# The recurrence of a four-layer kernel: conv by projection and diagonal taps, step sizes a group ahead with an operand in PSUM, keys in even slots

## The chip, the cores and the metric

The kernel runs on one core of one Trainium2 chip. Its time is the time of one execution in device microseconds (us). Five engines work side by side, each in the order of its own queue: PE multiplies matrices, DVE, ACT and POOL work element by element, SP issues DMAs. Data lies in SBUF (128 partitions) and in PSUM, which PE writes.

## What is computed

Four layers with residuals follow one another on x (4 sequences of 512 tokens, width 512, float32): a selective state-space layer driven by a context of width 256, a mixture of experts (64 experts, 8 per token), cross attention with 16 heads, and a feed-forward layer with quantized operands. The change concerns the first:

```
xc = causal_conv(in_proj_w @ ctx, conv_w)      # 4 taps per channel, 512 channels
u  = silu(xc + conv_b)
dt_lo, Bm, Cm = split(x_proj_w @ u)
delta = softplus(dt_proj_w @ dt_lo + dt_proj_b)
for each position:                             # 16 states per channel
    state = state * exp(delta * A) + (delta * u) * Bm
    y = sum over the states of state * Cm
out = (y + D * u) * silu(z)
```

The result is added to x; z comes from the normalized x. The keys and values of the attention layer depend on the context alone, so their projections are computed in part beside the first layer.

## The kernel before

The first layer is `ssm_phase`. Its instructions are written in the order in which each engine takes them; no scheduler changes it. The loop over `q` has 128 passes: sequence b (4, called batches), group of 128 channels c (4), pair of states i (8). One pass is called a slot here, and s is the slot within a batch (0 to 31). What a slot issues, in order:

- POOL multiplies du by the row of B for slot q + 2 (`inputs`, L518, into one of three buffers dBu).
- ACT makes exp(delta A) for slot q + 1 (`decays`, L529), into one of two PSUM buffers dA. Twice in a batch (`early`) it goes into an SBUF buffer ahead of its turn.
- DVE runs the scan along the positions (`scan`, L543); the product with the row of C is done by POOL for i = 0, 2, 4 and by DVE otherwise (L544, into one of three buffers hc).
- PE transposes the product of the slot before onto the PSUM tile yT, which adds up over the states (`sums`, L549). At i = 2 of the next group DVE multiplies yT by the gate (`result`, L583) and adds it to x (L586: on POOL, in the last batch on DVE). There is one yT.

Beside this each slot holds a piece of other work. `values` (PE L500, ACT L506, a store from SP) projects the values of attention in every second slot. The keys go through class `Keys`: `task` (PE L1227), `evict` (ACT L1236, L1237, a store), `squares` (PE L1247), `take` (ACT L1259, a store); 3, 6, 6 and 16 of them lie in the four batches, and nine more are computed later, in the expert layer (`key_tasks`).

`ahead` and `ahead_ends` prepare the next batch. For slots 0 to 15 PE computes the conv, two matmul calls a slot, from weights in which projection and taps are folded together (L320; a matmul call on float32 is two instructions in the profile). Then come the statistics of x (DVE), the norm (POOL L405 to L410), silu of u with two loads of ACT's tables (slot 17), the projection to B, C and dt (`project` L424, `take_project` L429), its store to DRAM by L430 and, from slot 26, the loads that spread its rows over the partitions (`rows`, L436, eight of 1024 KB a batch). In slots 19 to 28 the step sizes of all four groups of the next batch are made: `dt` (PE L443), `steps_a` (three on ACT), `steps_ln` (ACT L459, L462), `steps_b` (DVE L468, L469, L471) and `step_du` (POOL L479, L482). delta and du therefore have five buffers each, and u has six.

For batch 0 there is no time ahead: it projects by `conv_0`, applies the taps on DVE (`taps_0`, L351), and before and between makes the folded weights: `fold` scales the weights (DVE L371, ACT L369), `turn_fold` transposes them on PE (L378), `take_fold` copies them (L385, L387), `store_fold` writes them to DRAM, 512 KB for each group of channels; `load_wcv` (L310) reads them again for each batch. Its steps after the first group are in slots 1 to 12.

Of the kernel before, what the change touches and what calls it, by code (L numbers as in the profile page):

```python
# [24 lines left out]
ALU = mybir.AluOpType  # L25
# [215 lines left out]
def ssm_phase(ctx, cm, x_all, w, kv, router_stats):  # L241

    tc, nc = cm.tc, cm.nc
    pool = {n: ctx.enter_context(tc.tile_pool(name=f"a_p{n}", bufs=n)) for n in (1, 2, 3, 4, 5, 6)}
# [17 lines left out]
    def load_ctx(b, again=False):  # L264

        t = pool[2].tile([P, KC, S + DC - 1], F32, name="ctxb")
        nc.vector.memset(t[:, :, 0:DC - 1], 0.0)
        nc.sync.dma_start(t[:, :, DC - 1:],
                          w["ctxT"][:, b * S:(b + 1) * S].rearrange("(k p) s -> p k s", p=P))
        if again:  # L270
            st[b]["ctx"] = t
            return
        st[b] = dict(ctx=t, w=[], u=[], gz=[], delta=[], du=[], bb=[], cb=[],
                     mv=small.tile([P, NC, 2], F32, name="mv"))

    winT = pool[4].tile([P, KC, DM], F32, name="winT", tag="bb")
    nc.sync.dma_start(winT, w["in_proj_wT"].rearrange("(k p) e -> p k e", p=P))
    load_ctx(0)
    winE = pool[4].tile([P, NC, CTX], F32, name="winE", tag="cb")
    nc.sync.dma_start(winE, w["in_proj_w"].rearrange("(c p) k -> p c k", p=P))  # L280
# [24 lines left out]
    wcv_dram = dp.tile([NC, P, KC, DC, P], F32, name="wcv_dram")  # L305


    def load_wcv(b, c):
        t = pool[2].tile([P, KC, DC, P], F32, name="wcvc")
        nc.sync.dma_start(t, wcv_dram[c])  # L310
        st[b]["w"].append(t)

    def conv(b, c, parts):
        s = st[b]
        if 0 in parts:
            s["pin"] = ps.tile([P, S], F32, name="pin")
        for i in parts:
            k, j = divmod(i, DC)

            nc.tensor.matmul(s["pin"], s["w"][c][:, k, j, :], s["ctx"][:, k, j:j + S], start=i == 0,  # L320
                             stop=i == KC * DC - 1)

    def take_conv(b, c):
        u = pool[6].tile([P, S], F32, name="u")
        nc.scalar.activation(u, st[b]["pin"], AF.Identity, bias=vecs["conv_b"][:, c:c + 1])
        st[b]["u"].append(u)


    def conv_0(c):
# [3 lines left out]
        for k in range(KC):  # L333
            nc.tensor.matmul(pin, winT[:, k, c * P:(c + 1) * P], s["ctx"][:, k, DC - 1:],
                             start=k == 0, stop=k == KC - 1)

    def take_conv_0(c):
        s = st[0]
        xin = s["xin", c] = pool[2].tile([P, S + DC - 1], F32, name="xin", tag="wcvc")
        nc.gpsimd.memset(xin[:, 0:DC - 1], 0.0)  # L340
        pin = s.pop(("pin", c))
        nc.scalar.copy(xin[:, DC - 1:], pin)
        u = pool[6].tile([P, S], F32, name="u")
# [4 lines left out]
    def taps_0(c):  # L348
        xin, u = st[0].pop(("xin", c)), st[0]["u"][c]
        for j in range(DC - 1):  # L350
            nc.vector.scalar_tensor_tensor(u, xin[:, j:j + S], vecs["conv_w"][:, c, j:j + 1], u,  # L351
                                           ALU.mult, ALU.add)
# [5 lines left out]

    wsc = {}

    def fold(c):
        t = wsc[c] = pool[3].tile([P, DC, CTX], F32, name="wsc", tag="dBu" if c < 3 else "hc")
        for j in range(DC):
            scale = vecs["conv_w"][:, c, j:j + 1]
            if c == 3:
                nc.scalar.activation(t[:, j, :], winE[:, c, :], AF.Copy, scale=scale)  # L369
            else:  # L370
                nc.vector.tensor_scalar(t[:, j, :], winE[:, c, :], scale, None, ALU.mult)  # L371

    def turn_fold(c):
        t = wsc.pop(c)
        pt = wsc[c] = pda.tile([P, KC, DC, P], F32, name="pwcv", tag="dA")
        for k in range(KC):
            for j in range(DC):
                nc.tensor.transpose(pt[:, k, j, :], t[:, j, k * P:(k + 1) * P], cm.ident)  # L378

    def take_fold(c):  # L380
        pt = wsc.pop(c)
        t = wsc[c] = pool[4].tile([P, KC, DC, P], F32, name="wcv", tag="bb" if c % 2 else "cb")
        for k in range(KC):
            if c < 2:
                nc.scalar.copy(t[:, k], pt[:, k])  # L385
            else:
                nc.vector.tensor_copy(t[:, k], pt[:, k])  # L387

    def store_fold(c):
        nc.sync.dma_start(wcv_dram[c], wsc.pop(c))  # L390
# [21 lines left out]
    def silu_gz(b):  # L412
        s = st[b]
        for c in range(NC):
            gz = pool[5].tile([P, S], F32, name="gz")
# [30 lines left out]
    def steps_a(b):  # L446

        s = st[b]
        pdt = s.pop("pdt")
        s["e"], s["wt"] = (pool[1].tile([P, S], F32, name=n) for n in ("e", "wt"))  # L450
        s["relu"] = pool[5].tile([P, S], F32, name="delta")
# [4 lines left out]
    def steps_ln(b):  # L456

        s = st[b]
        nc.scalar.activation(s["wt"], s["e"], AF.Identity, bias=cm.ones[:, 0:1])  # L459
        s["ln"] = (pool[5].tile([P, S], F32, name="ln", tag="gz") if b == 0 else  # L460
                   ps.tile([P, S], F32, name="ln", tag="pin"))
        nc.scalar.activation(s["ln"], s["wt"], AF.Ln)  # L462

    def steps_b(b):

        s = st[b]
        e, wt, ln = s["e"], s["wt"], s["ln"]
        nc.vector.scalar_tensor_tensor(e, wt, 1.0, e, ALU.subtract, ALU.subtract)  # L468
        nc.vector.tensor_tensor(e, ln, e, ALU.subtract)  # L469
        delta = s.pop("relu")  # L470
        nc.vector.tensor_tensor(delta, delta, e, ALU.add)  # L471
        s["delta"].append(delta)

    def step_du(b):
# [3 lines left out]
        du = pool[5].tile([P, S], F32, name="du")  # L478
# [16 lines left out]
    def values(b, n, Wv):  # L495
        g, kc = divmod(n, S // P)
        pv = pvs[b, n] = ps.tile([P, HG * HD], F32, name="pv")
        at = slice(DC - 1 + kc * P, DC - 1 + (kc + 1) * P)
# [22 lines left out]
    def decays(q, early=False):  # L521

        if q < len(seq) and q not in dAs:
            b, c, i = seq[q]
            dAs[q] = (pool[2].tile([P, 2, S], F32, name="dA", tag="wcvc") if early else
# [55 lines left out]
    def result(b, c):  # L581
# [3 lines left out]

        (nc.vector if b == B - 1 else nc.gpsimd).tensor_tensor(xv, xv, t, ALU.add)  # L586

    def ahead(b, s):

        if s % 4 == 0 and 4 <= s <= 16:  # L590
            take_conv(b, s // 4 - 1)
        if s < 16:
            conv(b, s // 4, (s % 4 * 2, s % 4 * 2 + 1))
        if s in (4, 8):
            load_wcv(b, s // 4 + 1)
        if 12 <= s < 16:
            stats(b, s - 12)
        if s == 16:
            norm(b)
        if s == 17:  # L600
            silu_u(b)
        if s == 18:
            project(b)
        if s == 19:
            take_project(b)
        if s in (20, 22, 24, 26):
            steps_a(b)
        if s in (21, 23, 25):
            dt(b, (s - 19) // 2)
        if s in (22, 24, 26, 28):  # L610
            step_du(b)
        if s in (21, 23, 25, 27):
            steps_ln(b)
        if s == 29:
            silu_gz(b)
        if s == 20 and b + 1 < B:
            load_ctx(b + 1)
        if s == 20 and b + 1 == B:
            load_ctx(0, again=True)
        if s in (26, 28, 30, 31):  # L620
            rows(b, (26, 28, 30, 31).index(s))

    def ahead_ends(b, s):

        if s in (16, 28):
            decays((b - 1) * SL + s + 2, early=True)
        if s in (29, 31) and b + 1 < B:
            load_wcv(b + 1, (s - 29) // 2)
        if s == 19:
            dt(b, 0)  # L630
        if s in (21, 23, 25, 27):
            steps_b(b)
# [3 lines left out]
    def key_bank(shape, name):  # L636
# [1782 lines left out]
```

## Time and profile before

| | us |
|---|---|
| median of 3 runs | 2706.72 |
| lowest and highest | 2701.98 to 2717.91 |
| profiled execution | 2719.86 |
| its span in the profile | 2718.1 |
| end of the last product of the recurrence (L544) in the span | 577.1 |
| busy time of PE, DVE, POOL, ACT up to 577 | 492, 493, 476, 366 |
| mean granted clock of PE up to 577, and after | 0.90, 0.97 |

The profile is one execution. Busy time of an engine is the time in which it had an instruction in work; it says nothing on whether others waited for it. A window line gives, for a stretch of the span, the busy time and the number of instructions of each engine, then the granted clock of PE (1.00 is full), the share of time in which the DMA engines were busy, and what they moved. A line of an operation gives the least, the median and the greatest duration in ns. In a timeline line an idle time and what ended it stand in brackets.

### The profile page before, as it was taken

To read this page: it belongs to the slowest core of one execution; us is meant where nothing else is said; L and a number is where in the kernel's file an instruction comes from. 1 tells how busy PE (TensorE), PEld (TensorE's weight loads), DVE (VectorE), ACT (ScalarE), POOL (GpSimd) and SP (SyncE) were. 2 spreads that over 40 slices of the span, in tenths; PEclk is the share of its full clock that TensorE was granted. 3 is DMA by queue.
4 is the path that set the end of the run, shared out by engine and by line. 5 is a ranking of instruction groups with operands and counts; after the bars stand their busy time and mean duration, and the time that the engine had idled before them with its cause. 6 is when DMAs were issued, how large, how long until landed. Compare 5 with 4: busy or idle time off the path is not lost. (4 is left out here: it accounts for less than half of the span.)

```text
span 2718.1 us, 29941 instructions
## 1 busy us (share of the span) xinstructions
PE 2526.6 (93%) x10151; PEld 1432.6 (53%) x10151; DVE 1524.8 (56%) x2575; ACT 1237.6 (46%) x2355; POOL 1174.4 (43%) x1085
## 2 busy tenths in 40 slices
PE   5989797987799999999998799999999999999987
PEld 2545454654455666666674354445555555555543
DVE  5897989976322244344324555556665666544446
ACT  5666666655322222232322344444555455545543
POOL 4888888960333344443435423223332333211112
PEclk8979798988899999999998999999999999999999
DMA  6253535432656567879876444233332343222100
GB/s 247 90 196 104 199 105 183 125 124 98 196 189 210 185 221 219 288 264 321 283 222 215 130 134 128 90 100 110 125 101 86 109 128 113 75 76 66 51 31 20
DMA packets 199358, 404.67 MB, mean 149 GB/s; under 512 B 30611, under 2 KB 72147, under 8 KB 195104
## 3 DMA queue, kind: packets, MB, share of 16 engines
q1 hardware_dynamic: 156574, 249.33, 27.6%
q0 software_dynamic: 40576, 153.19, 17.7%
q8 instruction: 83, 1.36, 0.2%
q10 hardware_dynamic: 2050, 0.18, 0.1%
q14 instruction: 75, 0.61, 0.1%
HBM read 320.70 MB, written 81.92 MB: 148 GB/s over the span
## 5 line engine op out<-in xcount | busy, mean ns | idle before, releaser
L1981 DVE TENSOR_REDUCE mx<-psc 128x1 f32<-128x512 f32 x256 | 176.8, 691 | 459.6 <-PE psc L1978 459.6
L1327 PE MATMUL pg<-xT,wg 128*128 128x284 f32 (+12 forms) x1536 | 404.7, 408 | 1.4 <-ACT xT L1314 1.1
L1327 PEld LDWEIGHTS pg<-xT,wg 128*128 128x128 f32 x1536 | 285.4, 196 | 86.7 <-issue 36.9
L518 POOL TENSOR_TENSOR dBu<-bb,du 128x1024 f32<-128x1024 f32 x128 | 318.5, 2512 | 21.3 <-DVE dA L543 13.6
L1984 ACT ACTIVATE e<-psc,mx 128x512 f32<-128x512 f32 x256 | 176.1, 688 | 310.7 <-DVE mx L1981 310.4
L1268 POOL DMA_INDIRECT xg<-xn_dram,tok x168 | 172.8, 1028 | 219.5 <-PE pt L1311 177.4
L1978 PE MATMUL psc<-kT,qT 128*128 128x512 f32 x512 | 266.2, 602 | 1.0 <-ACT qT L1972 1.0
L2005 PE MATMUL po<-eT,v 128*128 128x512 f32 x512 | 233.2, 598 | 10.4 <-ACT eT L1999 10.3
L1944 PE MATMUL pq<-Wq,xnT 128*128 128x512 f32 x512 | 235.9, 604 | 0.7 <-DMA k_dram<-k_kT 0.7
L2014 PE MATMUL px<-Wo,oT 128*128 128x512 f32 x512 | 230.2, 592 | 0.0
L529 ACT ACTIVATE dA<-delta,negA 128x512 f32<-128x512 f32 x256 | 176.8, 694 | 79.1 <-DVE hc L544 62.2
L1998 PEld LDWEIGHTS pet<-ident,e 128*128 128x128 f32 x1024 | 127.0, 141 | 146.4 <-issue 119.6
L1955 POOL TENSOR_SCALAR qms<-qms 128x4 f32<-128x4 f32 x64 | 24.8, 388 | 413.6 <-DVE qms L1953 412.8
L543 DVE TENSOR_TENSOR_SCAN dA<-dA,dBu 128x1024 f32<-128x1024 f32 x80 | 184.8, 2311 | 17.2 <-POOL dBu L518 10.6
L549 PEld LDWEIGHTS yT<-ident,hc 128*128 128x128 f32 x1024 | 127.3, 151 | 92.1 <-issue 56.2
L549 PE MATMUL yT<-ident,hc 128*128 128x128 f32 x1024 | 142.8, 289 | 34.2 <-POOL hc L544 18.7
L1372 DVE COPY yo<-po 128x512 f32<-128x512 f32 x68 | 47.0, 691 | 220.3 <-PE po L1361 220.3
L2005 PEld LDWEIGHTS po<-eT,v 128*128 128x128 f32 x512 | 96.8, 191 | 137.7 <-issue 117.1
L1868 POOL DMA_INDIRECT yg<-y_dram,pos x124 | 125.2, 1010 | 86.0 <-issue 63.6
L1998 PE MATMUL pet<-ident,e 128*128 128x128 f32 x1024 | 154.2, 273 | 8.2 <-DVE e L1990 8.2
L1268 POOL DMA_INDIRECT wd<-down,widx x64 | 63.3, 990 | 204.6 <-PE po L1361 168.5
L1999 ACT COPY eT<-pet 128x512 f32<-128x512 f32 x256 | 148.2, 579 | 5.7 <-PE pet L1998 5.7
(356 smaller groups left out, 4459.3 us busy)
## 6 DMA issues: line engine op xcount, KB each, us to landing
y_dram<-yo SPq DMA_DIRECT2D x110, 256.0 KB
bb<-bc_dram SPq DMA_DIRECT2D x16, 1024.0 KB
cb<-bc_dram SPq DMA_DIRECT2D x16, 1024.0 KB
v_dram<-v SPq DMA_DIRECT2D x64, 256.0 KB
k_dram<-k_kT SPq DMA_DIRECT2D x64, 256.0 KB
Wq<-Wq SPq DMA_DIRECT2D x16, 1024.0 KB
kT<-k_dram SPq DMA_DIRECT2D x64, 256.0 KB
rk<-r_dram SPq DMA_DIRECT2D x64, 256.0 KB
```

Source lines behind the costliest of these rows:

```text
L518: nc.gpsimd.tensor_tensor(dBus[q], st[b]["bb"][i // 2][:, j:j + 2, :], st[b]["du"][c].unsqueeze(1).to_broadcast([P, 2, S]), ALU.mult)
L529: nc.scalar.activation(dAs[q][:, j, :], st[b]["delta"][c], AF.Exp, scale=negA[:, c, n:n + 1])
L543: nc.vector.tensor_tensor_scan(*flat, 0.0, ALU.mult, ALU.add)
L549: nc.tensor.matmul(yT[:, lc, :], t[:, lc * P:(lc + 1) * P], cm.ident, is_transpose=True, start=first and lc == 0, stop=last, skip_group_ch ...
L1268: nc.gpsimd.indirect_dma_start(out=t[0:n, :], out_offset=None, in_=table, in_offset=bass.IndirectOffsetOnAxis(ap=index, axis=0))
L1327: nc.tensor.matmul(pg[:, 0:n], s["wg"][:, c, m * P:(m + 1) * P], s["xT"][:, c, 0:n], start=c == 0, stop=c == NC - 1)
L1944: nc.tensor.matmul(pq.rearrange("p h d -> p (h d)"), xnTs[b * NC + i][:, c, :], s["Wq"][:, c, :], start=c == 0, stop=c == NC - 1)
L1978: nc.tensor.matmul(pscore, st[b, g]["qT"][:, h, i * P:(i + 1) * P], ks[n], start=True, stop=True)
L1981: nc.vector.tensor_reduce(mx, pscore, AX.X, ALU.max, negate=True)
L1998: nc.tensor.transpose(pt[:, kc, :], e[:, kc * P:(kc + 1) * P], cm.ident)
L2005: nc.tensor.matmul(po, v[:, kc, :], eT[:, kc, :], start=kc == 0, stop=kc == KB - 1)
L2014: nc.tensor.matmul(px, oTs[j * HG + h][:, i * P:(i + 1) * P], st[b, g]["Wo"][:, h, :], start=h == 0, stop=h == HG - 1)
```

## The change

- The conv of batches 1 to 3 is no longer folded into the projection. PE projects a group of channels (`project_in`, two matmul calls), ACT copies it to SBUF (`take_in`, into the one buffer xin), and four matmuls with diagonal matrices of the taps add up the conv (`conv`, one a slot). A group takes five slots, all four take slots 1 to 20. The diagonal matrices are made once, on POOL, from the identity (`make_taps`). Folding, its transposes, its store to DRAM and its loads are gone, the weights of the projection stay in SBUF.
- The step sizes are made one group ahead, also across the end of a batch: `dt` at i = 2, `steps_a` at i = 3, `steps_ln` and `steps_b` at i = 4, `step_du` at i = 5 of each group, for the next one. The tile pdt in PSUM is kept and written in place: ACT's 1 + e goes there, and each of DVE's three operations has it as an operand; ln lies in SBUF. delta and du have two buffers, u five, the gates four.
- silu of u moves from slot 17 to 23, the projection and its store from 18 and 19 to 23 and 24, the norm from 16 to 26, the statistics to 14, 16, 22 and 24, the first early decay from 16 to 22. The gate's transposes are at i = 1 in all groups.
- Keys: 5, 5, 5 and 16 in the batches, in even slots by a list (`plan_key`); their sums of squares share a PSUM bank with the values instead of with dt. The later nine are other heads, in the same number.
- The last batch's results are added on POOL too.

```diff
-    def load_wcv(b, c):
-        t = pool[2].tile([P, KC, DC, P], F32, name="wcvc")
-        nc.sync.dma_start(t, wcv_dram[c])
-        st[b]["w"].append(t)
-    def conv(b, c, parts):
+    taps = cp.tile([P, NC, DC, P], F32, name="taps")
+    xin = cp.tile([P, S + DC - 1], F32, name="xin")
+    nc.vector.memset(xin[:, 0:DC - 1], 0.0)
+    def make_taps(c):
+        for j in range(DC):
+            nc.gpsimd.tensor_scalar(taps[:, c, j, :], cm.ident, vecs["conv_w"][:, c, j:j + 1], None,
+                                    ALU.mult)
+    def project_in(b, c):
         s = st[b]
-        if 0 in parts:
-            s["pin"] = ps.tile([P, S], F32, name="pin")
-        for i in parts:
-            k, j = divmod(i, DC)
-            nc.tensor.matmul(s["pin"], s["w"][c][:, k, j, :], s["ctx"][:, k, j:j + S], start=i == 0,
-                             stop=i == KC * DC - 1)
+        s["pin"] = ps.tile([P, S], F32, name="pin")
+        for k in range(KC):
+            nc.tensor.matmul(s["pin"], winT[:, k, c * P:(c + 1) * P], s["ctx"][:, k, :],
+                             start=k == 0, stop=k == KC - 1)
+    def take_in(b):
+        nc.scalar.copy(xin[:, DC - 1:], st[b]["pin"])
+    def conv(b, c, j):
+        s = st[b]
+        if j == 0:
+            s["pin"] = ps.tile([P, S], F32, name="pc", tag="pin")
+        nc.tensor.matmul(s["pin"], taps[:, c, j, :], xin[:, j:j + S], start=j == 0, stop=j == DC - 1)
...
-    def fold(c):
-        t = wsc[c] = pool[3].tile([P, DC, CTX], F32, name="wsc", tag="dBu" if c < 3 else "hc")
-        for j in range(DC):
-            scale = vecs["conv_w"][:, c, j:j + 1]
-            if c == 3:
-                nc.scalar.activation(t[:, j, :], winE[:, c, :], AF.Copy, scale=scale)
-            else:
...
     def steps_ln(b):
         s = st[b]
-        nc.scalar.activation(s["wt"], s["e"], AF.Identity, bias=cm.ones[:, 0:1])
-        s["ln"] = (pool[5].tile([P, S], F32, name="ln", tag="gz") if b == 0 else
-                   ps.tile([P, S], F32, name="ln", tag="pin"))
-        nc.scalar.activation(s["ln"], s["wt"], AF.Ln)
+        nc.scalar.activation(s["pdt"], s["e"], AF.Identity, bias=cm.ones[:, 0:1])
+        s["ln"] = pool[1].tile([P, S], F32, name="ln", tag="yg")
+        nc.scalar.activation(s["ln"], s["pdt"], AF.Ln)
     def steps_b(b):
         s = st[b]
-        e, wt, ln = s["e"], s["wt"], s["ln"]
-        nc.vector.scalar_tensor_tensor(e, wt, 1.0, e, ALU.subtract, ALU.subtract)
-        nc.vector.tensor_tensor(e, ln, e, ALU.subtract)
-        delta = s.pop("relu")
-        nc.vector.tensor_tensor(delta, delta, e, ALU.add)
+        t, delta = s.pop("pdt"), s.pop("relu")
+        nc.vector.scalar_tensor_tensor(t, t, 1.0, s["e"], ALU.subtract, ALU.subtract)
+        nc.vector.tensor_tensor(t, s["ln"], t, ALU.subtract)
+        nc.vector.tensor_tensor(delta, delta, t, ALU.add)
         s["delta"].append(delta)
...
-        (nc.vector if b == B - 1 else nc.gpsimd).tensor_tensor(xv, xv, t, ALU.add)
+        nc.gpsimd.tensor_tensor(xv, xv, t, ALU.add)
     def ahead(b, s):
-        if s % 4 == 0 and 4 <= s <= 16:
-            take_conv(b, s // 4 - 1)
-        if s < 16:
-            conv(b, s // 4, (s % 4 * 2, s % 4 * 2 + 1))
-        if s in (4, 8):
-            load_wcv(b, s // 4 + 1)
-        if 12 <= s < 16:
-            stats(b, s - 12)
-        if s == 16:
-            norm(b)
-        if s == 17:
-            silu_u(b)
-        if s == 18:
-            project(b)
-        if s == 19:
-            take_project(b)
-        if s in (20, 22, 24, 26):
-            steps_a(b)
-        if s in (21, 23, 25):
-            dt(b, (s - 19) // 2)
-        if s in (22, 24, 26, 28):
-            step_du(b)
-        if s in (21, 23, 25, 27):
-            steps_ln(b)
-        if s == 29:
-            silu_gz(b)
+        if s in (2, 7, 12, 17):
+            take_in(b)
+        if s in (6, 11, 16, 21):
+            take_conv(b, s // 5 - 1)
+        if s in (14, 16, 22, 24):
+            stats(b, (14, 16, 22, 24).index(s))
         if s == 20 and b + 1 < B:
             load_ctx(b + 1)
         if s == 20 and b + 1 == B:
             load_ctx(0, again=True)
+        if s == 23:
+            silu_u(b)
+        if s == 24:
+            take_project(b)
+        if s == 26:
+            norm(b)
+        if s == 29:
+            silu_gz(b)
         if s in (26, 28, 30, 31):
             rows(b, (26, 28, 30, 31).index(s))
...
     def ahead_ends(b, s):
-        if s in (16, 28):
+        if s in (22, 28):
             decays((b - 1) * SL + s + 2, early=True)
-        if s in (29, 31) and b + 1 < B:
-            load_wcv(b + 1, (s - 29) // 2)
-        if s == 19:
-            dt(b, 0)
-        if s in (21, 23, 25, 27):
-            steps_b(b)
...
-    fold(3)
-    for c in range(3):
-        fold(c)
+        if 0 < s < 1 + NC * (1 + DC):
+            c, j = divmod(s - 1, 1 + DC)
+            project_in(b, c) if j == 0 else conv(b, c, j - 1)
+        if s == 23:
+            project(b)
...
+    def plan_key(q, b, h, bank):
+        key_at(q, True, key_task, b, h, bank)
+        key_at(q + 2, False, keys.evict)
+        key_at(q + 2, True, keys.squares)
+        key_at(q + 3, False, keys.take)
+    for b in range(B - 1):
+        for j, (s, bank) in enumerate(((6, "pa"), (14, "pa"), (22, "pin"), (26, "pin"), (30, "pin"))):
+            key_at(b * SL + s - 3, False, keys.load, j, j + 1, pool[2], "k_w")
+            plan_key(b * SL + s, b + 1, j, bank)
+    last_q = (B - 1) * SL
+    for h in range(H):
+        plan_key(last_q + 2 * h, 0, h, "pin")
+    for h, q in ((0, last_q - 8), (HG, last_q + 6), (2 * HG, last_q + 8), (3 * HG, last_q + 16)):
+        key_at(q, True, keys.load, h, h + HG, pool[2], "dA")
...
-        if q in (2, 4, 11):
-            steps_a(0)
-        if q in (3, 5, 12):
-            steps_ln(0)
-        late = 6 if c == NC - 1 or q < NP else 1
-        if i == late + 1:
+        if i == 2:
             take_gate(b, c)
+        to = seq[q // NP * NP + NP][0:2] if q + NP < len(seq) else None
+        if to is not None:
+            if i == 3:
+                steps_a(to[0])
+            if i == 4:
+                steps_ln(to[0])
+            if i == 5:
+                step_du(to[0])
...
-        if q in (1, 3, 10):
-            dt(0, len(st[0]["delta"]) + (q == 3))
-        if q in (3, 5, 12):
-            steps_b(0)
-            step_du(0)
+        if to is not None:
+            if i == 2:
+                dt(*to)
+            if i == 4:
+                steps_b(to[0])
...
-    left = [(b, h) for b in (2, 3) for h in (6, 7)] + [(1, h) for h in range(3, H // 2)]
+    left = [(b, h) for b in (2, 3, 1) for h in range(5, H // 2)]
```

## The prediction

> **What bounds the kernel now.** I read first the busy tenths in 40 slices (68 us each), to find where the change can act at all.
>
> ```profile
> PE   5989797987799999999998799999999999999987
> DVE  5897989976322244344324555556665666544446
> POOL 4888888960333344443435423223332333211112
> ```
>
> The diff touches the recurrence (slices 0 to 8, to 577 us) and, of the later part, only which heads' keys stay for it: nine before and after. There PE, DVE and POOL are all at 8 or 9, so no share of the span tells which one binds. I therefore cut the recurrence into groups (8 scans, one group of 128 channels) at the starts of the scans in the timeline, and asked for busy time by window. These are the four groups of the second sequence (batch 1), then one group of the last.
>
> ```profile
> core 0: us, PE busy (x) PEld busy (x) DVE busy (x) ACT busy (x) POOL busy (x), PEclk, DMA share, GB/s
> 190.80:220.10 29.30, 29.30 (x126) 17.27 (x127) 24.61 (x16) 18.35 (x31) 29.30 (x14) 1.00 0.51 172
> 220.10:253.80 33.70, 33.70 (x145) 19.82 (x144) 27.67 (x23) 18.02 (x30) 27.72 (x13) 1.00 0.38 121
> 253.80:293.40 39.60, 34.19 (x146) 19.80 (x144) 31.60 (x22) 26.71 (x44) 32.24 (x18) 0.91 0.20 62
> 293.40:330.10 36.70, 27.21 (x98) 16.47 (x98) 35.55 (x22) 24.86 (x38) 34.03 (x18) 0.72 0.74 269
> 493.40:522.60 29.20, 26.74 (x132) 18.06 (x131) 28.65 (x17) 18.79 (x34) 26.31 (x12) 0.88 0.35 111
> ```
>
> Each group has another limit. The second is PE alone: busy 33.70 of 33.70. The fourth is DVE, busy 35.55 of 36.70. The third mixes waits. A group of the last sequence, with no conv and no steps, runs in 29.2. What DVE does in the third and fourth is seen in the operation lines (min/median/max):
>
> ```profile
> L468 DVE SCALAR_TENSOR_TENSOR e<-wt,e x16: 692/1303/2899, 32.9 to 447.8; 128x512 f32<-128x512 f32 x16
> L469 DVE TENSOR_TENSOR e<-ln,e x16: 691/692/2654, 33.7 to 449.2; 128x512 f32<-128x512 f32 x16
> L471 DVE TENSOR_TENSOR delta<-delta,e x16: 691/1924/1959, 34.4 to 449.9; 128x512 f32<-128x512 f32 x16
> L518 POOL TENSOR_TENSOR dBu<-bb,du x128: 2334/2366/4346, 36.7 to 570.3; 128x1024 f32<-128x1024 f32 x128
> ```
>
> L469 reads ln from PSUM (in SBUF only for batch 0, which has its long case) and stays at 0.69; L468 and L471 have two SBUF operands and take up to 2.9. Last, the start, in the timeline and the waits of POOL:
>
> ```profile
> 28.64 0.68 ACT L429 ACTIVATE xd<-pd,ident 64x512 f32<-64x512 f32 x1 [4.50 <-PE pd L424]
> POOL dBu L518 <- DMA bb<-bc_dram: 7.7, 1, 7.7
> DVE dA L543 <- ACT dA L529: 2.7, 1, 2.7
> ```
>
> **What the Trainium skill says.** "SBUF — State Buffer", section "SBUF: two separate sides": DVE and GpSimd share a port pair as an exclusive lock, which a DVE operation with two SBUF inputs takes for its whole length against a GpSimd operation that reads SBUF; the other blocks. The trace agrees: 0.69 in PSUM form against a median of 1.92 for L471, and dBu up to 4.35 against 2.37. "TensorE: Matmul & The Clock Gate", section "HAM oscillation", says that gaps in PE's work bring its clock down. It agrees: 1.00 in the group with PE full, 0.72 in the fourth. So a relieved PE gets slower again; this caps what PE can give.
>
> **The change, part by part.** Names: a slot is one pass of the loop, a group 8 slots, a batch 32. First scans of batches 0 to 3 stand at 39.1, 190.8, 330.1 and 466.5, the recurrence ends at 577.1: batches of 151.7, 139.3, 136.4 and 110.6.
>
> *Conv.* Out: 32 matmuls of two instructions, 0.43 each (pitch in the timeline), 1.72 per slot for 16 slots, 27.5 a batch. In: 4 x (2 projections + 4 taps) = 24 matmuls, 20.6, over 20 slots. Check on the second group: conv 13.8, values 6.9, sums 8 x 0.87 = 7.0, Du and gate 0.9, two keys at 1.72 + 0.82 = 5.1; sum 33.7, as measured. After: one projection and seven taps 7.7 + 6.9 + 7.0 + 0.9 + one key 2.5 + dt 1.05 = 26.1, under the other engines. Keys per batch go from 3, 6, 6, 16 to 5, 5, 5, 16. Added on ACT: four copies to xin at 0.58 (row L342), 2.3 a batch on an engine with 88 of 139 busy.
>
> *Steps.* Per group of channels DVE's three operations go from 1.48 + 0.81 + 1.39 = 3.7 to 3 x 0.69 at pitch 0.72 = 2.1, since each has one operand in PSUM. The same count of them, but one set in each group, and three sets move from batches 0 to 2 into batch 3 (batch 0 loses three: four instead of seven in its loop).
>
> *POOL, next in line.* Per group 8 dBu at pitch 2.33, 3 hc at 2.31, the result's add 1.27, du and reset 1.3: 28.1. Per batch also norm 2.2 and the two early dA in SBUF, which hold POOL by 1.9 (two dBu in 6.58 instead of 4.67, at 399.4) and 2.8 (four in 12.1 instead of 9.3, at 182.1). DVE per group: 3 x 2.20 + 5 x 3.53 + result 0.6 + steps 2.1 = 27.0, and 0.88 per statistics. So POOL is late next.
>
> *Waits added.* In slot 4 of a group L468 waits for L459, which on ACT stands behind the next dA (1.4) and, where a key is evicted, 1.27; behind L468 on DVE wait L469, L471 and the next scan, and for those POOL's dBu. dA of slot 5 starts when scan 4 does, so L459 ends 2.1 to 2.3 after that, beside scan 4's 2.28: at least nothing. With steps_a (1.7) and the conv's copies ahead on ACT I estimate 1.2 a group; bounds 0 and 2.7, the longest wait of L468 for L459 in the loop of the trace of before (15 x 1.5 = 22 us more). Conv tap 0 waits on PE for xin, with sums queued behind it; PE has 2 us of room a group, so I take nothing. kpss moves to the bank of pv, so PE's squares wait for v's copy (L506) and the next values for L1259, with sums behind both: in batch 3 the copy ends some 3.3 us into a slot pair of 7, and PE's own work in the pair is 6.5; I take nothing, and 1 a group of batch 3 if it shows.
>
> *Table loads.* silu_u moves from slot 17, a short slot on DVE (2.2), to slot 23, where slots of 3.53 cover its 4.75 us on ACT; the 2.7 us wait for dA goes; next late there is POOL. With it xd and its store to bc_dram move from slot 19 to 24, ahead of the bb and cb loads of slot 26 on SP: the store took 1.7 at the start (29.4 to 31.0), two slots are 5.7, so nothing; without that cover, bb has still four slots until slot 30 reads it. norm's four POOL operations move from slot 16 to 26, into the fourth group, which POOL bounds; that is in its sum. The gate's transposes come in slot 1 of every group, beside PE's wait for the result that frees yT.
>
> Sums by batch, in groups: first and second 28.1 + 1.2 = 29.3; third 30.2 with its two statistics; fourth is POOL's, 28.1 + 2.2 + 4.7 = 35.0. Together 123.8, saving 15.5 and 12.6 in batches 1 and 2.
>
> *Start.* The fold goes: 2.0 of ACT and DVE ahead of the taps (xin copied at 10.9 though its matmuls end near 9.3), two copies of 1.1 ahead of the last silu, and 32 transposes ahead of pd. Taps take 9.2 as before and end near 20, silu at 20.9, pd near 22.2 instead of 28.6: 6.4 earlier. Added: 16 small POOL operations, 0.3 to 0.5 each by the nearest rows, beside DVE's taps; POOL is idle there for 11.6. Were they to hold the taps, 12 x 0.5 = 6 at most. Two stores and two loads of 512 KB leave SP's queue ahead of the second bb; with 3.5 MB instead of 5.5 ahead and included, I take its wait from 7.7 to 2.4. Batch 0: 30.5 + 29.3 + 30.2 + 35.0 = 125.0, saving 26.7. Twelve later loads of wcv go from SP's queue; nothing waited for them after the first.
>
> *Last batch.* 3 x 30 (with evictions ahead of L459) + 24.9 without steps = 114.9: 4.3 more. The result's add on POOL is 1.27, not 0.67: 0.6 at the end. Three adds that took 4.36, 3.57 and 1.26 on DVE are within POOL's 28.1.
>
> Sum: -6.4 - 26.7 - 15.5 - 12.6 + 4.3 + 0.6 = -56.3. The profiled execution took 2719.86 (span 2718.1 and 1.8 around it), so 2663.6; it lies 13.1 over the median of the runs, so 2650 in their terms. All after 577 us waits for this stage and moves with it.
>
> **Rivals.**
> *Overlap is nearly perfect* (16%): L459 is never late, POOL keeps its 119 in batches 0 to 2, and DVE's L471 no longer holds it. For: the last sequence's groups ran at their engine's sum, 29.2 and 28.4. Gain 73 to 78: 2632.
> *PSUM operands don't free the port* (8%): each of 15 sets keeps its 1.6, 24 us back: 2674. Against: L469's 692. For: L468's in-place form in PSUM isn't in the trace; I bound it by 0.69 and today's mean of 1.48.
> *Hand-overs cost more* (13%): PE, with gaps, falls to 0.7 of its clock in all groups, its chain projection, copy, tap, dt is late, 2.5 a group: 38 back, 2688.
> *Slower* (6%): steps close a ring in each group: PE's dt behind sums, steps_a behind it on ACT, dA of slot 5 behind that, L459, then DVE. If PE is a slot late (3.5) in slot 2, ACT waits with dA queued behind, and DVE waits in slot 4. From 4.7 over my estimate in each of 15 groups (70 us) it passes the old time by 0.5%: 2722. Against: dt's inputs are ready a group ahead.
>
> **How the numbers follow.** The main case (57%) covers 2638 to 2664. Most of the first rival lies above 2628 and of the third below 2690: range 2628 to 2690, leaving out some two in ten. A measurement here tells about 0.5%, 13.5 us, from no change. Of the third rival's 13%, 6 lie below 2693, 6 within 0.5% and 1 above. Faster: 57 + 16 + 8 + 6 = 87%; within 0.5%: 6%; slower: 1 + 6 = 7%.
>
> **What would show it.** First scan near 32.7; second bb waited for by under 4; groups of batches 1 and 2 near 29 with the fourth near 35 and POOL full in it; L468, L469, L471 all at 0.69 to 0.8; PE below 30 of each group; no wait of a scan for yT over 1; batch 3 some 4 longer. The prediction is wrong if L468 waits for L459 by more than 3 in most groups, if PE's clock is under 0.8 in the first two groups of a batch, or if POOL's dBu still has a mean near 2.5.

## The result, and the profile after

The changed kernel took 2674.12 us (median of 4 runs, 2660.34 to 2679.07), the kernel before 2712.31 (median of 4, 2701.98 to 2718.23): a ratio of 0.9855 with a 95% interval of 0.9827 to 0.9883, 38 us or 1.4% faster. The forecast was 2650, 56 us faster, with a range of 2628 to 2690, which holds the time.

The profiled execution took 2669.67 (span 2668.0) after 2719.86 (span 2718.1), 50 less. Not all of that is the change. The recurrence ends at 534.3 instead of 577.2, 42.9 earlier. What follows it takes 2133.7 instead of 2140.9, but in a further profile of the changed kernel (below) it took 2139.4 with the recurrence ending at 535.0, and over the eleven profiles of the changed kernel and of the edits of it below, whose code after the recurrence is the same, it went from 2124.0 to 2143.8. So the 7 us of the rest are within the spread of single executions, and the study is about 43 us where 56 were foretold. The experiments are judged by the end of the recurrence first and by the ratio second. The end lay within 1 us in the two profiles of the changed kernel, but single groups in them differ by up to 3.3, so a difference of 4 or 5 us between single profiles is a weak sign.

The busy tenths after, in 40 slices of 67 us:

```profile
PE   6989898977999999999997899999999999999987
...
DVE  6889888955232443344316545456665666554446
...
POOL 7899999822233444444326233123422433221112
```

In the first eight slices POOL is now at 9 in five, PE and DVE at 8 and 9 from the second on: still three engines near full, and again not to be told apart here. The windows tell more: the second to fourth group of the second sequence, the first of the third, and one of the last sequence.

```profile
core 0: us, PE busy (x) PEld busy (x) DVE busy (x) ACT busy (x) POOL busy (x), PEclk, DMA share, GB/s
192.30:223.10 30.80, 30.39 (x136) 17.85 (x134) 27.21 (x21) 18.90 (x32) 28.19 (x15) 1.00 0.32 99
223.10:252.80 29.70, 27.02 (x120) 15.65 (x121) 27.95 (x23) 24.03 (x39) 28.13 (x15) 1.00 0.27 89
252.80:285.80 33.00, 25.61 (x117) 14.76 (x115) 30.73 (x21) 25.15 (x41) 30.09 (x18) 0.95 0.78 291
285.80:318.40 32.60, 29.13 (x106) 17.29 (x107) 26.44 (x18) 19.46 (x33) 30.24 (x16) 0.79 0.27 94
447.00:477.60 30.60, 28.67 (x139) 18.27 (x138) 26.34 (x18) 21.15 (x39) 28.10 (x15) 0.94 0.34 106
```

PE is relieved as foretold in the third and fourth group (27.02 and 25.61 busy), though not in the second, where it has 30.39 of 30.80: there it makes up for the long group before it, with 20 instructions of values and 72 of sums where a group has 16 and 64. POOL's 28.19 and 28.13 are the foretold sum of 28.1. The fourth window is new: its PEclk is 0.79, where the group before has 0.95. Now the operations:

```profile
L442 DVE SCALAR_TENSOR_TENSOR pdt<-pdt,e x16: 698/699/700, 28.1 to 495.6; 128x512 f32<-128x512 f32 x16
...
L443 DVE TENSOR_TENSOR pdt<-ln,pdt x16: 695/696/697, 28.9 to 496.4; 128x512 f32<-128x512 f32 x16
...
L444 DVE TENSOR_TENSOR delta<-delta,pdt x16: 686/686/689, 29.6 to 497.1; 128x512 f32<-128x512 f32 x16
...
L491 POOL TENSOR_TENSOR dBu<-bb,du x128: 2338/2358/3141, 31.8 to 528.1; 128x1024 f32<-128x1024 f32 x128
```

All three of DVE's are at 0.69 to 0.70, with hardly any spread, and the longest dBu falls from 4.35 to 3.14 us. The copy behind the table load at the start and POOL's wait for the second bb:

```profile
23.27 0.68 ACT L403 ACTIVATE xd<-pd,ident 64x512 f32<-64x512 f32 x1
```

```profile
POOL dBu L491 <- DMA bb<-bc_dram: 1.2, 1, 1.2
```

xd comes at 23.27 instead of 28.64, and bb is waited for by 1.2 instead of 7.7. DVE's own waits in the recurrence (total, times, longest, in us) hold the surprise:

```profile
engine line waited for: us in total, times, longest us
DVE pdt L442 <- ACT ln L435: 37.5, 15, 5.7
DVE hc L516 <- ACT dA L502: 8.2, 4, 3.0
```

L442 waits in all of the 15 sets of the loop, 2.5 each on average, and the line named is L435. L442 reads pdt and e; ln, which L435 makes, is not among its operands. L442 writes pdt in place, though, and L435 reads pdt: a wait named after an instruction that makes none of the waiter's operands suggests one for the place, not for the data. ln_from_e below tests this.

By the terms of the prediction, from the starts of the first scans (34.2, 159.9, 285.8 and 412.5; groups in brackets, in us):

| | before | foretold | after | after: groups |
|---|---|---|---|---|
| first scan | 39.1 | 32.7 | 34.2 | |
| batch 0 | 151.7 | 125.0 | 125.7 | 30.8, 30.6, 31.3, 33.0 |
| batch 1 | 139.3 | 123.8 | 125.9 | 32.4, 30.8, 29.7, 33.0 |
| batch 2 | 136.4 | 123.8 | 126.7 | 32.6, 31.4, 29.7, 33.0 |
| batch 3 | 110.6 | 114.9 | 121.8 | 34.5, 30.6, 30.7, 25.9 |

Of the shortfall of 13, half is in batch 3, and the first groups of batches 1 to 3 stand out.

### The profile page after: what moved, and what is told of

The parts are those of the page before. It is cut to its first block, busy times and chain, and to the rows that moved or that the text cites. A ratio compares the mean times of both kernels' runs of the same rounds, so it can differ in the third digit from the quotient of the medians.

```text
span 2668.0 us, 29715 instructions
## 1 busy us (share of the span) xinstructions
PE 2493.4 (93%) x10071; PEld 1411.5 (53%) x10071; DVE 1485.6 (56%) x2551; ACT 1234.9 (46%) x2359; POOL 1178.0 (44%) x1105
## 5 line engine op out<-in xcount | busy, mean ns | idle before, releaser
L491 POOL TENSOR_TENSOR dBu<-bb,du 128x1024 f32<-128x1024 f32 x128 | 302.0, 2375 | 18.8 <-DVE dA L516 17.1
L522 PEld LDWEIGHTS yT<-ident,hc 128*128 128x128 f32 x1024 | 120.7, 145 | 82.2 <-issue 38.1
L522 PE MATMUL yT<-ident,hc 128*128 128x128 f32 x1024 | 135.8, 280 | 18.4 <-DVE hc L517 14.5
```

The costliest lines, as they stand in the source:

```text
L491: nc.gpsimd.tensor_tensor(dBus[q], st[b]["bb"][i // 2][:, j:j + 2, :], st[b]["du"][c].unsqueeze(1).to_broadcast([P, 2, S]), ALU.mult)
L522: nc.tensor.matmul(yT[:, lc, :], t[:, lc * P:(lc + 1) * P], cm.ident, is_transpose=True, start=first and lc == 0, stop=last, skip_group_ch ...
```

## The experiments

All are edits of the changed kernel. The theory: the gain comes from the operand in PSUM and from the lighter conv and start; what is missing went into L442's wait, made by the place of L433 and L435 in ACT's queue and by the write in place, and, in the first group of a batch, into a slower PE. The rivals: that the conv alone gave the gain, and that POOL's sum is the floor, so that an earlier Ln brings nothing. Open besides was whether the late projection or PE's clock lengthens first groups. The kernel before was timed again beside each set of runs, and each ratio is to those times. The end comes from one profile of each run.

| run | ratio to before | end of the recurrence |
|---|---|---|
| changed kernel | 0.9855 [0.9827, 0.9883] | 534.3 |
| after_again | 0.9837 [0.9799, 0.9874] | 535.0 |
| sbuf_operand | 0.9993 [0.9979, 1.0008] | 577.8 |
| folded | 0.9902 [0.9874, 0.9929] | 555.1 |
| proj_slot0 | 0.9817 [0.9791, 0.9842] | 530.4 |
| pe_filled | 0.9814 [0.9781, 0.9846] | 523.9 |
| ln_from_e | 0.9806 [0.9769, 0.9844] | 518.9 |
| ln_slot3 | 0.9731 [0.9703, 0.9758] | 506.1 |
| ln3_e_proj0 | 0.9739 [0.9700, 0.9778] | 505.9 |
| ln3_no_early | 0.9712 [0.9677, 0.9748] | 501.2 |
| ln3_e_no_early | 0.9725 [0.9695, 0.9756] | 496.6 |

### The operand in PSUM, undone

In 11 of the 15 sets of the loop 1 + e lies in SBUF (two lines more, so L442 to L444 become L444 to L446).

```diff
-    def steps_ln(b):
+    def steps_ln(b, sbuf=False):
         s = st[b]
+        if sbuf:
+            s["pdt"] = pool[2].tile([P, 2, S], F32, name="wt", tag="dA")[:, 0, :]
...
-                steps_ln(to[0])
+                steps_ln(to[0], q < 2 * SL + 3 * NP)
```

> The changed kernel, but in 11 of the 15 step sets of the loop (slots 4, 12, 20 and 28 of batches 0 and 1, slots 4, 12 and 20 of batch 2) the tile with 1 + e lies in SBUF instead of PSUM; the other sets stay. Theory (the port): L442, L443 and L444 go from 0.70 each to a mean of 1.2 to 1.5 in these sets, dBu's mean rises from 2.375, each set costs 1.5 to 2, and the recurrence ends 15 to 22 us later than in the changed kernel (549 to 556 instead of 534). Rival (the spread): the gain came from having one set in each group and not from where the operand lies; the recurrence ends within 4 us of 534.

The whole gain is gone: ratio 0.9993, end 577.8. The two forms stand beside one another in one run (least, median, greatest in ns):

```profile
L444 DVE SCALAR_TENSOR_TENSOR wt<-wt,e x11: 956/1811/2932, 54.1 to 405.1; 128x512 f32<-128x512 f32 x11
L444 DVE SCALAR_TENSOR_TENSOR pdt<-pdt,e x5: 699/700/700, 28.3 to 539.2; 128x512 f32<-128x512 f32 x5
L445 DVE TENSOR_TENSOR wt<-ln,wt x11: 692/2724/2732, 56.8 to 406.9; 128x512 f32<-128x512 f32 x11
L445 DVE TENSOR_TENSOR pdt<-ln,pdt x5: 695/695/697, 29.1 to 539.9; 128x512 f32<-128x512 f32 x5
```

The PSUM form stays at 0.70 in all five; the SBUF form has medians of 1.81 and 2.72 in the first two operations. And POOL waits for DVE in turn, 38.3 in all instead of 17.1 (total, times, longest):

```profile
POOL dBu L493 <- DVE dA L518: 38.3, 32, 2.0
```

A second or third group with an SBUF set takes 34.9 to 35.2, one without 30.6 or 30.7: 4.4 a set, since DVE loses 3.1 in the operations themselves and POOL's products come late on top. The end is 43.5 later, about twice what I expected (15 to 22). The form here is a little worse than that of the kernel before, where L469 still read ln from PSUM. And wt takes a buffer of those for the early dA; but in second groups no early dA is written or read, and they lose no less than third groups, so the buffer is not what they lose by.

### The conv, undone

Folded weights, their loads and the two calls per slot of the kernel before, in the changed kernel (lines move by 25):

```diff
-        if s in (2, 7, 12, 17):
-            take_in(b)
-        if s in (6, 11, 16, 21):
-            take_conv(b, s // 5 - 1)
+        if s % 4 == 0 and 4 <= s <= 16:
+            take_conv(b, s // 4 - 1)
+        if s < 16:
+            conv(b, s // 4, (s % 4 * 2, s % 4 * 2 + 1))
...
-        if 0 < s < 1 + NC * (1 + DC):
-            c, j = divmod(s - 1, 1 + DC)
-            project_in(b, c) if j == 0 else conv(b, c, j - 1)
```

> The changed kernel with the conv of before: folded weights, made, stored and loaded again as before, eight matmuls for a group of channels in slots 0 to 15; steps, keys and all else as changed. Theory (two parts, steps the larger): the first scan is 6 later and its second bb waited for by 4 more, PE has 32 of work in the first two groups, which take 32 to 33; the recurrence ends 12 to 18 us later (546 to 552), so conv and start are a third to 40% of the 43 us that the change took off the recurrence. Rival (conv is the main part): PE is the limit again and the recurrence ends at 562 or later.

```profile
POOL dBu L516 <- DMA bb<-bc_dram: 7.8, 1, 7.8
```

End 555.1: 20.8 later than the changed kernel, of which the start has 4.7, batch 0 8.5 with the wait for bb of 7.8 back, batches 1 and 2 4.6 and 3.4. I expected 546 to 552, so the conv and its weights were worth some more. What remains of the change beside them, the steps, silu, norm and keys, gives the other 22 together (577.2 to 555.1). The parts do not add: without PSUM 43.5 are lost, without the conv 20.8.

### L433 and L435 a slot earlier

```diff
                 steps_a(to[0])
-            if i == 4:
                 steps_ln(to[0])
```

> The changed kernel with steps_ln issued in slot 3, right behind steps_a, instead of in slot 4 behind the next dA and the key's evictions. Theory (ACT's order is on the path): L442's wait for L435 falls from 37.5 in the loop to under 15, the groups go from 30.7 to 29.5, batch 3 most, and the recurrence ends 12 to 20 us earlier (514 to 522). Rival (POOL binds): the same waits go over to scans that wait for dBu, POOL being busy for 28 of 30.7 in a group, and the recurrence ends less than 5 us earlier.

```profile
DVE pdt L442 <- ACT ln L435: 11.2, 10, 2.2
```

The wait falls from 37.5 to 11.2, by 26.3, and the end by 28.2, to 506.1, further than I expected (514 to 522): most of this wait had been on the path. The two don't match group by group. In the fourth groups of batches 0 to 2 the wait of 1.65 goes, or falls to 0.77, and the groups stay (32.8 to 33.3, for 33.0). In the first groups of batches 1 to 3 the wait falls by 8.4 and the groups by 10.7, with a PEclk of 0.94 where the changed kernel had 0.79 and 0.80. Groups two and three now take 28.4 to 28.7, which is POOL's sum of 28.1 and a little.

### L435 reads e instead of pdt

Ln of e with a bias of 1 gives the same value without pdt, so nothing but L433 stands ahead of the write in place.

```diff
-        nc.scalar.activation(s["ln"], s["pdt"], AF.Ln)
+        nc.scalar.activation(s["ln"], s["e"], AF.Ln, bias=cm.ones[:, 0:1])
```

> The changed kernel with L435 reading e in SBUF, with a bias of one, instead of pdt, which L442 writes in place; order and slots stay. Theory (in place costs a wait): L442 may then start when L433 has ended and not when L435 has read pdt, 0.7 to 1.0 earlier in each of 15 sets, and the recurrence ends 8 to 14 us earlier (520 to 526). Rival (only the order counts): L443 waits for L435 in its place, as it needs ln, and the recurrence ends less than 4 us earlier.

```profile
DVE pdt L442 <- ACT pdt L433: 27.4, 15, 4.8
```

The wait is now named after L433 and falls to 27.4; the end falls by 15.4, to 518.9 (expected 520 to 526). So the hazard is real: 10.1 of 37.5, or 0.7 a set, is L442 waiting until L435 has read what L442 will overwrite. The other 1.8 a set are L433's own place in the queue. That the end gained more than the wait fell goes with the first groups of batches 1 to 3, which are 6.5 shorter together at a PEclk of 0.94, 0.89 and 0.84.

### Projection at slot 0

```diff
-        if 0 < s < 1 + NC * (1 + DC):
+        if s == 0:
+            project_in(b, 0)
+        if 1 < s < 1 + NC * (1 + DC):
```

> The changed kernel with the first projection of each batch at the end of slot 0 instead of slot 1, so that it doesn't stand behind PE's wait for yT. Theory (hand-over): ACT's wait of 5 for the projection, with dA behind it, goes in batches 1 and 2, with DVE's 3.0 for dA; the first group falls from 32.5 to 30, and the recurrence ends 5 to 9 us earlier. Rival (clock): the first group is long because PE's granted clock is 0.79 there; it stays at 32 and the recurrence ends within 3 us of 534.

ACT's waits for pin (13.8 in the changed kernel) and three of DVE's four waits for dA (8.2 to 1.7) go, but L442's stay and the end is 530.4, 4 earlier: less than the 5 to 9 expected, more than the rival's 3. First groups of batches 1 and 2 take 31.3 and 31.5 at a PEclk of 0.84, inside the spread of the changed kernel's two profiles (30.5 to 32.6). So the run doesn't show the late projection to be the root of the long first groups.

### The changed kernel again

No edit.

> The changed kernel once more, for its time beside that of the others of this set and for how much a second profile differs. Theory: the groups of the recurrence repeat within 1 us each and its end within 3 us of 534; what comes after it took 2134 against 2141 before, which I put down to PE's granted clock and not to the change, so here it lies anywhere between 2125 and 2141. Rival (the later part gained too, from other keys): it takes 2134 within 2 us again.

End 535.0, L442's waits 39.0. Ten of the 16 groups repeat within 0.2. The first groups of batches 1 to 3 take 30.5, 32.2 and 33.2 at a PEclk of 0.94, 0.89 and 0.90, where the first profile had 32.4, 32.6 and 34.5 at 0.79, 0.79 and 0.80. Against that the first group of batch 0 takes 32.5 instead of 30.8 and the third of batch 1 33.0 instead of 29.7; the second of batch 2 takes 30.2 instead of 31.4. I had expected all to repeat within 1. That the two ends agree to 0.7 is thus partly chance.

### Work added to PE

In the last three slots of batches 0 to 2, two matmul calls whose result nobody reads, 12 instructions a batch (about 5 us).

```diff
+        if s in (29, 30, 31):
+            t = ps.tile([P, S], F32, name="fill", tag="pa")
+            for n in range(2):
+                nc.tensor.matmul(t, winT[:, 0, 0:P], st[b]["ctx"][:, 0, :], start=True, stop=True)
```

> The changed kernel with two more matmul calls, whose result nobody reads, at the end of each of slots 29, 30 and 31 of batches 0 to 2 (1.7 us of PE each at full clock). Theory (clock): PE's granted clock in the first groups of batches 1 to 3, 0.79 to 0.80, rises above 0.9, ACT waits less there for PE, and those groups lose 1 to 3 each. Rival (order): those groups are long since ACT stands behind PE's chain whatever the clock; they stay within 1, or grow by the added work.

The first groups of batches 1 to 3:

```profile
core 0: us, PE busy (x) PEld busy (x) DVE busy (x) ACT busy (x) POOL busy (x), PEclk, DMA share, GB/s
159.58:188.73 29.15, 27.34 (x118) 15.39 (x117) 26.39 (x18) 19.31 (x33) 29.09 (x16) 1.00 0.33 111
283.17:312.32 29.15, 27.09 (x116) 15.11 (x115) 26.39 (x19) 19.32 (x33) 29.09 (x16) 1.00 0.33 114
405.79:436.69 30.90, 29.09 (x136) 18.06 (x135) 26.38 (x18) 21.15 (x39) 30.26 (x16) 0.94 0.41 135
```

With more to do, PE has its full clock there in two of three groups, and the groups take 29.15, 29.15 and 30.90, 3.3 to 3.6 less, which is more than the 1 to 3 expected. Over the three profiles each of the three groups is the shorter the higher its clock. The end is 523.9, 10.4 earlier, and these three groups account for it. In the median (2658.91, ratio 0.9814) this isn't told apart from the repeat's 0.9837, whose interval overlaps; the stage alone shows it.

### Without the early dA in SBUF, on top of the earlier Ln

```diff
-        if s in (22, 28):
-            decays((b - 1) * SL + s + 2, early=True)
```

> The changed kernel with steps_ln in slot 3, and without the two early decays of each batch: all dA lie in PSUM. Theory (the port): POOL loses 4.7 a batch less to scans and products that have two operands in SBUF, but ACT's two stretches with table loads (4.75 and 5.5) hold dA back by some 3 each; the fourth groups go from 33.2 to 31 or 32 and the recurrence ends 3 to 7 us earlier than with early decays (499 to 503). Rival (the early decays pay): the scans wait for dA by more than the port costs, and it ends later than 506.

```profile
L491 POOL TENSOR_TENSOR dBu<-bb,du x128: 2338/2360/2389, 31.3 to 495.1; 128x1024 f32<-128x1024 f32 x128
```

```profile
DVE pdt L442 <- ACT ln L435: 12.3, 10, 3.1
DVE dA L516 <- ACT dA L502: 8.8, 6, 3.4
DVE hc L516 <- ACT dA L502: 3.9, 2, 2.3
```

No dBu is over 2.39 any more (4.35 in ln_slot3, 3.14 in the changed kernel), and fourth groups take 30.1 to 32.2 instead of 32.8 to 33.3. In exchange DVE's scans wait 12.7 for dA (8.8 and 3.9) instead of 1.7, the thing the early ones were there for. Net 4.9 earlier than ln_slot3, 501.2 (expected 499 to 503), from one profile of each; the ratios, 0.9712 and 0.9731, have overlapping intervals.

### Two sets of three edits together

Earlier Ln, Ln from e, projection at slot 0:

> The three edits together: steps_ln in slot 3, L435 reading e, the first projection of a batch in slot 0. Theory (POOL is the floor now, 28.1 a group and 34 in the fourth): little is left to gain, 1 to 5 us under the 506 of steps_ln in slot 3 alone, from L442's remaining 11 us and the first groups' 29.5. Rival (DVE's waits were all on the path): the 11 us come off in full, 495 or less.

```profile
DVE dA L516 <- POOL dBu L491: 9.8, 12, 1.6
DVE pdt L442 <- ACT pdt L433: 5.8, 7, 2.5
```

L442's wait is down to 5.8 and the end is that of ln_slot3, 505.9, where 1 to 5 less was expected: DVE now waits for POOL's products in 12 places, and POOL is busy 463.84 of the stage's 471.9. Beyond ln_slot3, shortening the steps' wait gives nothing while the early dA lengthen POOL's products.

Earlier Ln, Ln from e, no early dA:

> The changed kernel with steps_ln in slot 3, L435 reading e, and no early decays. Theory (POOL is the floor): 0 to 4 us under the 501 of the same without the second edit, groups of 28.5 where nothing is loaded on ACT. Rival (DVE's remaining 12 us of waiting for L435 are on the path): 490 or less.

The earliest end, 496.6, 4.6 before ln3_no_early (0 to 4 expected), with POOL busy 449.68 of 462.9. By ratio the four kernels with the earlier Ln (0.9712 to 0.9739) aren't told apart, as their intervals overlap; all four beat the kernel before and the changed one.

## Why the prediction was right in sign and too large

**Start: nearly right.** 4.9 came of 6.4. The fold's removal shows as foretold: xd 5.4 earlier, bb waited for by 1.2 instead of the foretold 2.4. The missing part is ahead of the taps: I let the copy to xin start near 9.3, where its matmuls ended before; it waits for PE until 10.53 now. PE's own first matmul waits for the load of the context until 7.11, where it was 6.79 before; why the rest is later stays open. The 16 tap operations on POOL took 0.60 to 0.91 each, more than the 0.3 to 0.5 that I gave them, and were hidden as assumed.

**Conv: right in the main; batch 0: right in its sum.** 26.0 of 26.7 came for batch 0, by luck in part: its groups were foretold at 30.5, 29.3, 30.2 and 35.0 and took 30.8, 30.6, 31.3 and 33.0. Undoing the conv, with its part in the start, costs 20.8, about half of the gain. PE was to be under 30 in each group, 26.1 in a second one; it had 30.39 in the second of batch 1 and 31.74 in the first of batch 3.

**PSUM operand: right, and the rival against it mispriced.** The 0.69 to 0.70 of all three operations and dBu's mean of 2.38 (foretold: no longer near 2.5; before 2.51) hold. This agrees with the Trainium skill's "SBUF — State Buffer", section "SBUF: two separate sides", by which a DVE operation with two SBUF inputs takes the port pair against a GpSimd operation that reads SBUF; with one input in PSUM, 0.70 stands here beside running products. I priced the loss of it at 1.6 a set from the operations alone; in the run it was 4.4 a group, because the other engine loses too. That the median of 2674.12 meets this rival's 2674 is chance, since the three operations did fall to 0.69 to 0.70.

**The step that failed: "In slot 4 of a group L468 waits for L459", 1.2 a group.** L468 is now L442, L459 is L433. It waits for more than that: for L435 as well, since the write is in place. I had read the operands of L442, and not who else reads the tile that it writes. The wait is 2.5 a set (8.6, 8.1, 8.1 and 12.7 us in the four batches): 2.0 to 2.2 in the first three batches, and 4.2, beyond the upper bound of 2.7, in the last. Of the 19.5 over the 18 foretold (15 × 1.2), 10.1 is the write in place, by ln_from_e, and the other 9.4 the queue ahead of L433. In the last batch ACT's queue holds the evictions of keys ahead of L433, in the changed kernel's timeline (start, duration, then the line; in brackets the idle time and what ended it):

```profile
428.10 0.17 ACT L1196 ACTIVATE k_ms<-kpss 128x4 f32<-128x4 f32 x1 [1.88 <-PE kpss L1184]
428.17 0.71 ACT L540 ACTIVATE Du<-u,v_D 128x512 f32<-128x512 f32 x1
428.78 0.59 ACT L426 ACTIVATE e<-pdt 128x512 f32<-128x512 f32 x1
429.26 0.60 ACT L427 ACTIVATE delta<-pdt 128x512 f32<-128x512 f32 x1
429.73 0.64 ACT L428 ACTIVATE e<-e 128x512 f32<-128x512 f32 x1
430.25 1.42 ACT L502 ACTIVATE dA<-delta,negA 128x512 f32<-128x512 f32 x2
431.61 0.58 ACT L1173 ACTIVATE k_sq<-pk 128x512 f32<-128x512 f32 x1
432.09 0.68 ACT L1174 ACTIVATE k_kT<-pk,gkq 128x512 f32<-128x512 f32 x1
432.66 0.69 ACT L433 ACTIVATE pdt<-e,ones 128x512 f32<-128x512 f32 x1
433.72 0.60 ACT L435 ACTIVATE ln<-pdt 128x512 f32<-128x512 f32 x1 [0.37 <-ACT pdt L433]
```

Only 0.37 is idle in these six us after the first line: ACT works through Du, steps_a, two dA and two evictions before it comes to L433 and L435. The queue began late, too: k_ms had waited 1.88 for PE's squares (kpss), one of 11 such waits of 15.2 in all (9 of 13.5 before), which the prediction's sums leave out. In pe_filled DVE's wait at this place is 3.98. In the changed kernel DVE stands for 5.74:

```profile
434.35 0.70 DVE L442 SCALAR_TENSOR_TENSOR pdt<-pdt,e 128x512 f32<-128x512 f32 x1 [5.74 <-ACT ln L435]
...
436.42 2.29 DVE L516 TENSOR_TENSOR_SCAN dA<-dA,dBu 128x1024 f32<-128x1024 f32 x1
```

I had allowed for evictions in batch 3 with 30 instead of 29.3 a group. Batch 3 took 121.8 instead of 114.9, 11 more than before where 4 were foretold. That most of the wait is on the path, and not beside POOL's work, ln_slot3 shows: 26.3 less of it brought 28.2.

**First groups: a rival came true in one group each of batches 1 to 3.** The rival of costlier hand-overs named PE at 0.7 of its clock in all groups; it was 0.79 and 0.80 in the first group of batches 1 to 3 of the profiled execution. There the projection of values, 1.88 for four instructions elsewhere, took 3.62, and the rest of the chain is seen behind it:

```profile
291.54 3.62 PE L473 MATMUL pv<-Wv,ctxb 128*128 128x512 f32 x4
...
296.66 1.91 PE L317 MATMUL pin<-ctxb,winT 128*128 128x512 f32 x4
...
298.61 0.59 ACT L321 COPY xin<-pin 128x512 f32<-128x512 f32 x1 [5.09 <-PE pin L317]
...
299.56 1.43 ACT L502 ACTIVATE dA<-delta,negA 128x512 f32<-128x512 f32 x2
...
301.08 2.29 DVE L516 TENSOR_TENSOR_SCAN hc<-dA,dBu 128x1024 f32<-128x1024 f32 x1 [2.97 <-ACT dA L502]
```

pin ends at 298.57, ACT has waited 5.09 for it with dA queued behind, and the scan at 301.08 has waited 2.97 for dA. That is the trace's "hand-over". proj_slot0 takes out these waits and gains little; pe_filled adds work to PE and gains 10.4. So the lower clock is the likelier root. It follows the fourth group, where PE has 25.61 busy of 33.00: by windows of 4 us the clock was 0.50 from 288 to 296, and in pe_filled it was 1.00 from 281.2 to 297.2. By the section "HAM oscillation" of the Trainium skill's "TensorE: Matmul & The Clock Gate", idle gaps of more than about 3.4 us bring PE's clock down. The trace agrees in the direction and not in the length: the longest gap between 252 and 292 was 2.44 us, from 283.46, where PE waited for DVE's product. What else the added calls shift was not told apart. Of my own list of what would prove the forecast wrong, "PE's clock is under 0.8 in the first two groups of a batch" came half true.

**Fourth groups: 33.0 instead of 35.0.** POOL is busy 30.1 in them: the norm's 2.2 came, the 4.7 for early dA in SBUF did not, as the longest dBu of 3.14 shows. It was DVE that took longer, in the two scans of early dA and in a product, which took 2.28 and 1.22 elsewhere:

```profile
252.78 3.34 DVE L516 TENSOR_TENSOR_SCAN hc<-dA,dBu 128x1024 f32<-128x1024 f32 x1
...
276.20 3.96 DVE L516 TENSOR_TENSOR_SCAN dA<-dA,dBu 128x1024 f32<-128x1024 f32 x1
280.27 2.04 DVE L517 TENSOR_TENSOR hc<-dA,cb 128x1024 f32<-128x1024 f32 x1
```

That is 3.6 more on DVE, whose 30.73 in this group is now above POOL's 30.09. The early dA cost the group 1 to 3, by ln3_no_early. So two errors in opposite directions made the sums of batches 0 to 2 look better than their parts were: the first and second were foretold too short, by 0.3 to 3.3 (batch 1: 29.3 twice, for 32.4 and 30.8), the fourth too long by 2. The third's 30.2 holds 0.88 once, though two statistics lie in it; it took 31.3, 29.7 and 29.7.

**Sum.** Shortfalls in the stage: start 1.5, batches 0.7, 2.1, 2.9 and 6.9, less the 0.6 for the tail: 13.5, which is the 56.3 foretold against 42.9 but for rounding. The 19.5 that L442 waits over the forecast are more than this; the fourth groups gave 6.0 back.

## What to carry to other kernels

An operand in PSUM was worth far more here than the shorter operation, in a loop in which DVE and POOL are both near full: price both engines' loss. When an operation is made to write in place, list everyone who reads that tile, not only its own operands, and look at what stands in the queue ahead of those readers; issuing the readers one slot earlier gave back 28 us here for a move of one call. PE's clock was 0.79 behind its emptiest group, so a relieved PE is better costed at the clock of its emptier groups than at full speed.

## What the runs showed of the hardware that was not expected

- Two DVE operations with both inputs in SBUF, beside POOL's products, took 1.81 and 2.72 us at the median where the form with one PSUM operand took 0.70, and a group lost 4.4 us to it.
- Adding about 5 us of unread matmuls to PE ahead of a sequence's end went with a clock of 1.00, 1.00 and 0.94 instead of 0.79, 0.79 and 0.80 in the groups that follow, and with groups shorter by 3.3, 3.5 and 3.6 us (against the repeat: 1.4, 3.0 and 2.3).
- PE's granted clock stood at 0.50 for about 8 us (288 to 296) though the longest gap in PE's work in the 36 us before was 2.44 us.
- A POOL tensor_scalar of 128x128 with a scalar per partition took 0.60 to 0.91 us (median 0.78), a third of the 2.36 of a product eight times its size.
